# A graph network over 16 graphs: the nodes' transpose moved from TensorE to VectorE's 32x32 blocks

## The chip, the core and the metric

The kernel runs on one core of a Trainium2 chip. The metric is the device time of one execution in microseconds (us); lower is better. A core has five engines that run their own instruction queues in order: TensorE (PE, matrix products, with weight loads shown apart as PEld), VectorE (DVE), ScalarE (ACT), GpSimd (POOL) and SyncE (SP, which here only issues transfers). They wait for one another by semaphores.

## What is computed

For each of 16 graphs there are 1024 nodes with 256 features (x, fp32) and a symmetric adjacency matrix of 1024 x 1024 (int32, here 0 or 1, with ones on the diagonal). Layer 0 gates the sum over neighbours by a sigmoid of a weighted product of the nodes; layer 1 is graph attention with four heads. After each layer the input is added and the rows are normalised.

```python
h = hidden
e0 = leaky(einsum('bid,bjd->bij', h * a0[:, 0], h))      # e1, e2, e3 alike, for adj 2, 3, 4
alpha = sigmoid(where(adj == 1, e0, neg_inf))
x = layernorm(x + einsum('bij,bjd->bid', alpha, h) + bias)

Wh = (x @ W).reshape(B, N, H, F)                         # H = 4, F = 64
e = leaky_relu(e_src[:, :, None, :] + e_dst[:, None, :, :], 0.2)
alpha = softmax(where(mask, e, NEG_INF), axis=2)
x = layernorm(x + elu(einsum('bijh,bjhf->bihf', alpha, Wh)))
```

Since the adjacency is symmetric and holds only 0 and 1, the fast path uses e0 alone and computes only the upper half of the scores; a check at the end of the program falls back to a general path if the data don't allow this. The general path isn't taken with these inputs.

## The kernel before

Rows of 1024 nodes are held as 8 blocks of 128 partitions, features as two chunks of 128. The product of all nodes with all nodes needs x twice: with nodes on the partitions (tile xb, also the operand of the aggregation) and with features on the partitions (tile xT). The way from one to the other is what changes.

A graph is a set of stages, Python generators inside `stages` that issue one step at each `next`. In order of a graph's data:

- `xload` (L248) loads xb, `aload` (L258) the adjacency by blocks; `cast` (ScalarE) makes it bf16, `turn` (L281) transposes it (by transfer from SP, except in the first graph), `mask` (ScalarE) keeps it as bytes (mT).
- `xt` (L311) turns xb on TensorE: 16 transposes of 128x128 (L319) into four PSUM banks. `xtc` (L324) copies each bank to xT on ScalarE (L330). `xta` (L336) multiplies by a0 (ScalarE, L344).
- `score` (L352, products at L356), `leak` and `leaky` (slope 0.2, ScalarE L368 and VectorE L376), `sigmoid` (ScalarE L382), `below` and `lower` (L395, L401: mirror the upper half), `upper` (L412), `self_loop` (L419).
- `agg` (L423, products at L427), `residual` (L459), row statistics, `norm0` (ScalarE L489), `yt` (transposes L498), `ytc` (ScalarE L507), `project` (L513, L517), `wh` (ScalarE).
- `top_dve` and `top_pe` find a common maximum; the first step of top_dve (span, L560) reads all that wh has copied. `exps`, `product`, `high` and `low` make the factors (gm); `sload` (L644) brings the rows of sources (sbc).
- `pos` (L654, VectorE L658) makes a 0/1 matrix per head and block, 64 steps a graph; `acc` (products at L670) and `total` (L713) sum over it; `acc_low` (ScalarE L685) and `acc_sum` (VectorE L693) empty PSUM; then division, ELU (ScalarE L816), join, second normalisation and `leave` (store).

What sets the order on each engine is a table written out: TIMES gives each stage's steps a time in a graph's own count, FIRST and LAST do so for the first and last graph. `issue` (L1229) adds PERIOD (112.0) times the graph's number, sorts all steps, and issues them in that order. The units are a plan's, not measured microseconds; only the order counts, as every engine runs its queue in order. So three graphs are in flight at a time: scores of the next graph, attention of this one, the finish of the one before.

Buffers that matter: xb has two (pool f_io), xT one that it shares with yT (pool f_big), PSUM four banks for pt, e, agg, pw, pg, tot and the like (f_ps_t) and two double banks for acc, pos six.

```python
for b, stages in enumerate(graphs):
    table = FIRST if b == 0 else LAST if b == len(graphs) - 1 else TIMES
    for name, times in table.items():
        steps += [(b * PERIOD + at, stages[name]) for at in times]
for _, stage in sorted(steps, key=lambda step: step[0]):
    next(stage)
```

Of the kernel before, what the change touches and what calls it, by code (L numbers as in the profile page):

```python
# [27 lines left out]
P = 128  # L28
# [4 lines left out]
class Consts:  # L33
    pass

# [50 lines left out]
def transposed(nc, k, pl, src, name, copy, tag=None):  # L86

    dstT = pl.big.tile([P, k.DC, k.N], F32, tag=tag or name, name=name)
    for c in range(k.DC):
        for g in range(k.NH):  # L90
            pt = pl.ps_t.tile([P, 4, P], F32, tag="pt", name="pt")
            for q in range(4):
                nc.tensor.transpose(pt[:, q, :], src[:, 4 * g + q, c * P : (c + 1) * P], k.ident)
            copy(
                dstT[:, c, g * HALF : (g + 1) * HALF], pt.rearrange("p q n -> p (q n)")
            )
    return dstT
# [96 lines left out]
def stages(nc, k, pl, b, xg, adjg, outg, sums, span, zinv):  # L194
# [26 lines left out]
    def setup():  # L221
# [7 lines left out]
        nc.sync.dma_start(out=k.w_aug[:, :, 0:D], in_=w.rearrange("(c p) f -> p c f", p=P))  # L229
# [11 lines left out]
        for i in range(1, NK):  # L241
            nc.sync.dma_start(
                out=k.a_sb[:, :, i : i + 1], in_=a_list[i].rearrange("(c p) o -> p c o", p=P)
            )
# [3 lines left out]
    def xload():  # L248
# [7 lines left out]
        yield  # L256

# [53 lines left out]
    def xt():  # L311
        if first:

            t["acol"] = bank("acol")
            nc.tensor.transpose(t["acol"][:, 0:DC], k.a_row, k.ident[0:DC, 0:DC])
        for c, half in PARTS:
            pt = t["xt", c, half] = quads("pt")
            for q in range(NQ):
                nc.tensor.transpose(  # L319
                    pt[:, q, :], t["xb"][:, half * NQ + q, c * P : (c + 1) * P], k.ident  # L320
                )
            yield

    def xtc():  # L324
        t["xT"] = pl.big.tile([P, DC, N], F32, tag="xT", name="xT")
        if first:
            nc.vector.tensor_copy(k.a_sb[:, :, 0], t["acol"][:, 0:DC])
        for c, half in PARTS:
            copy = nc.vector.tensor_copy if first and c == 0 else nc.scalar.copy
# [163 lines left out]
    def yt():  # L493
        for half in range(NH):
            for c in range(DC):
                pt = t["yt", half, c] = quads("pt")
                for q in range(NQ):
                    nc.tensor.transpose(  # L498
                        pt[:, q, :], t["y", half][:, q, c * P : (c + 1) * P], k.ident
# [370 lines left out]
    def leave():  # L870
# [11 lines left out]
        setup=setup(), xload=xload(), aload=aload(), cast=cast(), turn=turn(), mask=mask(),  # L882
# [20 lines left out]
    "xload": [-190.36],  # L903
    "aload": [-141.21, -134.94, -129.14, -126.41, -107.72, -95.92, -52.91, -49.35],
    "cast": [-133.33, -126.54, -110.85, -106.42, -72.33, -55.28, -40.89, -29.41],
    "turn": [-133.00, -118.97, -108.09, -86.35, -62.89, -45.14, -38.49, -26.07],
    "mask": [-126.25, -118.09, -94.06, -70.56, -52.12, -40.03, -32.69, -25.15],
    "setup": [-54.43, -50.76, -47.38],
    "xt": [-69.63, -66.83, -65.59, -61.38],
    "xtc": [-65.35, -64.69, -63.96, -57.76],  # L910
    "xta": [-60.02, -56.47, -53.23, -47.62, -40.80, -39.84, -35.73, -22.45],
    "score": [
        -55.95, -54.26, -52.86, -52.85, -50.30, -47.61, -41.77, -41.05, -37.61, -36.60,
        -31.53, -19.69,
    ],
    "leak": [
        -54.25, -52.28, -52.05, -51.99, -45.24, -41.19, -38.48, -36.59, -34.23, -28.07,
        -26.47, -19.19,
    ],
    "leaky": [  # L920
        -53.92, -51.61, -45.43, -45.41, -41.52, -40.38, -37.19, -36.20, -32.91, -26.88,
        -25.80, -17.05,
    ],
    "sigmoid": [-50.37, -36.56, -28.45, -23.28, -23.17, -15.81, -5.09, 4.38],
    "below": [-43.48, -40.73, -36.17, -28.75, -25.55, -24.80, -21.22, -11.11, 7.22, 7.95],
    "lower": [-41.97, -37.35, -33.23, -27.18, -24.41, -23.38, -19.01, -9.26, 8.37, 17.62],
    "upper": [-24.74, -21.21, -20.88, -18.06, 1.37, 12.57, 17.16, 22.61],
    "self_loop": [-22.52, -20.95, -18.10, -17.88, 3.26, 14.07, 18.13, 24.49],
    "agg": [
        -18.25, -16.27, -15.06, -15.02, -4.11, -4.03, -2.54, 0.32, 5.09, 8.13, 15.85,  # L930
        17.47, 21.46, 23.59, 23.78, 24.56,
    ],
    "residual": [-8.35, -7.46, -1.27, 2.37, 22.46, 22.48, 26.43, 27.74],
    "moments0": [-5.49, -4.53, 5.61, 8.01, 23.75, 25.11, 27.16, 28.13],
    "gathered0": [4.13, 6.42, 7.91, 10.51, 26.40, 27.32, 28.51, 29.05],
    "spread0": [13.40, 31.26],
    "shift0": [17.29, 31.54],
    "norm0": [21.66, 21.89, 22.47, 23.38, 34.53, 34.91, 35.50, 35.54],
    "yt": [27.46, 27.57, 36.68, 36.99],
    "ytc": [29.00, 29.33, 39.29, 39.57],  # L940
    "project": [32.52, 32.60, 33.90, 39.19, 40.28, 40.33, 40.41, 40.81],
    "wh": [33.22, 36.59, 37.58, 40.10, 40.68, 42.17, 42.34, 43.12],
    "sources": [41.16, 45.78],
    "rows": [41.83, 54.07],
    "keep_rows": [44.82, 56.53],
    "top_dve": [43.38, 45.01, 45.39, 50.81, 51.81],
    "top_pe": [44.42, 46.92],
    "exps": [51.81],
    "product": [53.02, 53.37, 53.98, 54.66, 58.34, 66.43, 69.20, 72.08],
    "high": [53.76, 54.40, 58.33, 58.56, 61.32, 68.49, 71.81, 73.63],  # L950
    "low": [54.19, 57.97, 61.74, 62.89, 71.04, 72.63, 75.29, 76.96],
    "sload": [50.80, 79.07, 83.92, 88.62, 102.34, 116.17, 128.36, 142.07],
    "pos": [
        57.31, 58.08, 60.13, 63.67, 69.85, 70.05, 71.57, 77.68, 80.69, 81.39, 82.09,
        82.79, 83.51, 84.84, 85.08, 85.50, 94.75, 97.25, 97.29, 97.48, 99.31, 100.22,
        100.86, 101.86, 104.39, 105.08, 105.66, 107.42, 108.55, 108.94, 109.06, 109.44,
        111.06, 112.18, 112.18, 112.50, 114.43, 114.99, 117.57, 118.23, 118.61, 122.99,
        125.51, 126.22, 128.00, 128.98, 130.58, 132.32, 133.80, 134.68, 135.40, 135.59,
        136.35, 141.70, 144.45, 144.66, 145.90, 146.60, 148.13, 149.39, 151.16, 153.05,
        156.93, 159.83,  # L960
    ],
    "acc": [
        66.06, 67.27, 68.14, 69.24, 71.32, 72.44, 73.71, 78.80, 83.16, 83.97, 84.72,
        85.39, 85.74, 87.50, 88.94, 90.52, 99.28, 99.52, 100.60, 101.24, 101.47, 101.85,
        102.15, 102.38, 108.43, 108.66, 109.45, 109.46, 109.72, 110.12, 110.70, 110.77,
        114.66, 115.11, 115.34, 116.25, 116.73, 118.20, 118.35, 119.33, 130.24, 130.46,
        130.54, 131.53, 132.09, 132.57, 134.85, 134.91, 141.46, 142.49, 142.93, 144.35,
        145.14, 145.81, 145.91, 146.87, 153.97, 154.83, 159.23, 159.59, 164.73, 165.20,
        165.32, 166.33,
    ],  # L970
    "acc_low": [
        79.49, 79.83, 96.76, 97.23, 103.47, 104.76, 112.24, 112.31, 122.02, 122.21,
        134.93, 135.59, 149.34, 149.98, 169.77, 170.85,
    ],
    "acc_sum": [
        80.66, 80.96, 97.10, 98.04, 105.15, 105.96, 112.53, 112.54, 127.47, 127.48,
        136.59, 136.70, 149.39, 150.00, 171.97, 175.58,
    ],
    "all_edges": [
        24.35, 76.79, 79.33, 79.88, 81.06, 82.66, 85.63, 89.08, 96.83, 101.38, 102.99,  # L980
        108.02, 111.52, 113.15, 116.96, 118.15,
    ],
    "total": [
        77.14, 77.24, 78.75, 79.22, 79.40, 79.41, 79.97, 80.39, 84.60, 84.83, 85.08,
        85.73, 89.40, 89.80, 90.91, 93.34, 97.93, 100.95, 101.71, 106.58, 107.02, 107.21,
        109.68, 110.76, 112.06, 113.36, 114.66, 114.68, 117.04, 118.18, 118.28, 119.92,
    ],
    "total_kept": [80.79, 83.22, 90.91, 93.71],
    "total_less": [112.64, 113.12, 119.31, 124.40],
    "weigh": [119.49, 129.29, 190.71, 191.25, 196.08, 212.23],  # L990
    "divide": [
        125.16, 126.39, 127.60, 129.50, 130.49, 134.23, 134.70, 134.85, 200.68, 201.14,
        206.69, 213.74, 214.56, 214.57, 216.22, 218.60,
    ],
    "elu": [133.27, 142.72, 214.93, 220.17],
    "join": [136.57, 142.87, 142.93, 145.63, 220.24, 222.78, 225.82, 228.23],
    "moments1": [146.58, 148.42, 152.65, 153.15, 223.48, 227.82, 229.78, 230.58],
    "gathered1": [146.81, 150.62, 154.63, 154.74, 228.81, 229.65, 230.64, 230.81],
    "spread1": [164.98, 232.04],
    "shift1": [165.77, 237.22],  # L1000
    "norm1": [195.74, 197.90, 202.92, 203.03, 238.05, 240.07, 240.16, 240.29],
    "leave": [206.44, 240.93],
    "weigh_end": [222.86, 228.40],
    "divide_end": [222.94, 223.01, 223.09, 223.17, 228.57, 228.75, 228.92, 229.09],
    "elu_end": [223.25, 229.26],
    "join_end": [223.32, 223.40, 229.44, 229.61],
}
FIRST = {
    "aload": [-146.50, -146.40, -145.60, -145.40, -145.20, -144.50],
    "cast": [-146.00, -145.00, -144.10, -143.30, -142.40, -141.30, -140.80, -140.10],  # L1010
# [467 lines left out]
```

## Time and profile before

| what | value |
|---|---|
| median of 3 runs | 1741.87 us (1741.26 to 1742.15) |
| span of the profiled execution, first to last instruction | 1739.6 us |
| median of the runs less that span | 2.27 us |
| TensorE busy | 1692.1 us, 97% |
| VectorE busy | 1639.6 us, 94% |
| ScalarE busy | 1239.4 us, 71% |
| GpSimd busy | 106.8 us, 6% |
| mean granted TensorE clock | 0.990 |
| share of the 16 DMA engines' time, SP's queue | 36.1% |

The page gives no other time of the profiled execution than its span; what lies around the span is taken from the runs. Groups in the profile are lines of the kernel: engine, operation, output<-inputs, shapes, count, then busy time and mean duration of one instruction, then the idle time of the engine before them and who ended it. A wait line reads: engine, tile and line that waited, what it waited for, then the sum in us, how many times, and the longest. Busy time is the union of instructions that overlap, so a mean duration is longer than the pace at which the instructions follow each other. The ends of matrix products are modelled, so that a busy TensorE can also hide short waits; the chain of waits and the list of waits say more there.

### The profile page before, as it was taken

Reading aid. Unit: us, or ns where it says so; the run is one execution under the profiler, and the core shown is the slowest. Engines: PE = TensorE matmul, PEld = TensorE weight load, DVE = VectorE, ACT = ScalarE, POOL = GpSimd, SP = SyncE. Lnnn points to the kernel's source line nnn. Section 1 sums busy time; section 2 is a strip of 40 time slices with the busy share of each in tenths; the row PEclk is TensorE's granted clock in tenths of the full one; section 3 lists DMA queues with packets and bytes.
Section 4 is the critical chain, followed back from the end, with each engine's and each line's share of the span. In section 5 each row is a group of like instructions: output and inputs, shape, how many; then the busy total and the mean of one; then the engine's idle time right before and its main releaser. Section 6 shows DMA issues by size and latency. Waiting matters only on the chain.

```text
span 1739.6 us, 29647 instructions
## 1 busy us (share of the span) xinstructions
PE 1692.1 (97%) x10580; PEld 1492.5 (86%) x10580; DVE 1639.6 (94%) x3663; ACT 1239.4 (71%) x2766; POOL 106.8 (6%) x138
## 2 busy tenths in 40 slices
PE   8999999999999999999999999999999999999984
PEld 5789898998979889898998979889898898979883
DVE  5498999999999999999999999999999999999998
ACT  7674957759587685967759587685967859586784
POOL 0000000010000101000010000101000010000100
PEclk9999999999999999999999999999999999999987
DMA  5542333434334343333435334443343424422020
GB/s 190 129 116 67 98 98 92 110 92 131 88 89 101 105 125 92 94 101 92 109 92 129 91 86 102 105 128 91 89 107 92 110 67 117 105 71 55 26 68 26
DMA packets 249005, 168.59 MB, mean 97 GB/s; under 512 B 133010, under 2 KB 232468, under 8 KB 248852
## 3 DMA queue, kind: packets, MB, share of 16 engines
q1 hardware_dynamic: 248848, 166.63, 36.1%
q8 instruction: 86, 1.41, 0.3%
q14 instruction: 67, 0.55, 0.1%
q10 hardware_dynamic: 4, 0.00, 0.0%
HBM read 118.10 MB, written 17.04 MB: 78 GB/s over the span
## 4 chain that ended last, share of the span: by engine, by line
PE 91%; DVE 3%; ACT 2%; DMA 1%; issue 1%; POOL 0%; SPq 0%; ACTq 0%; DVEq 0%; POOLq 0%
PE acc L670 27%; PE agg L427 24%; PE tot L713 14%; PE e L356 13%; PE pw L517 7%; PE pg L395 3%; PE pt L498 2%; PE pt L319 1%; DVE pos L658 1%; DMA sbc<-sdram 1%; ACT prod L614 0%; DMA aT<-a 0%; PE pbc L591 0%; ACT gm L633 0%; ACT y L489 0%
## 5 line engine op out<-in xcount | busy, mean ns | idle before, releaser
L658 DVE SCALAR_TENSOR_TENSOR pos<-sbc,nd,mT 128x512 fp32r<-128x512 f32 x1024 | 737.4, 745 | 10.5 <-PE acc L670 5.0
L670 PE MATMUL acc<-gm,pos 128*128 128x260 f32 x4096 | 608.6, 292 | 8.9 <-DVE gm L640 5.0
L670 PEld LDWEIGHTS acc<-gm,pos 128*128 128x128 f32 x4096 | 536.8, 190 | 19.8 <-issue 5.7
L427 PE MATMUL agg<-xb,gate 128*128 128x256 f32 x2048 | 463.5, 379 | 0.2
L427 PEld LDWEIGHTS agg<-xb,gate 128*128 128x128 f32 x2048 | 379.9, 190 | 47.6 <-DVE gate L419 1.2
L713 PE MATMUL tot<-gm,allm 128*128 128x264 f32 x2048 | 328.8, 297 | 5.4 <-ACT gm L633 4.9
L713 PEld LDWEIGHTS tot<-gm,allm 128*128 128x128 f32 x2048 | 281.4, 189 | 9.7 <-ACT gm L633 5.1
L356 PE MATMUL e<-xT,xTa 128*128 128x512 f32 (+3 forms) x768 | 264.3, 489 | 2.2 <-ACT xTa L344 1.4
L356 PEld LDWEIGHTS e<-xT,xTa 128*128 128x128 f32 x768 | 135.1, 191 | 106.4 <-issue 55.3
L685 ACT COPY low<-acc 128x260 f32<-128x260 f32 x256 | 89.8, 377 | 187.5 <-PE acc L670 187.3
L705 ACT CAST allm<-mT 128x512 fp32r<-128x512 uint8 x256 | 157.4, 615 | 33.4 <-PE tot L713 31.7
L489 ACT ACTIVATE y<-y,shift,rstd 128x256 f32<-128x256 f32 x254 | 136.3, 592 | 48.6 <-DVE shift L477 48.6
L276 ACT ACTIVATE a<-a 128x1024 bf16<-128x1024 int32 x124 | 131.3, 1059 | 32.1 <-DMA aT<-a 23.0
L298 ACT ACTIVATE mT<-aT 128x1024 uint8<-128x1024 bf16 x120 | 127.1, 1059 | 7.6 <-DMA aT<-a 7.5
L468 POOL TENSOR_SCALAR std<-mv 128x4 f32<-128x4 f32 x64 | 27.7, 432 | 1618.7 <-DVE mv L450 1447.1
L517 PE MATMUL pw<-w_aug,yT 128*128 128x264 f32 x512 | 121.8, 387 | 0.5 <-ACT yT L507 0.5
L376 DVE TENSOR_TENSOR gate<-e,gate 128x512 f32<-128x512 f32 x192 | 105.5, 556 | 14.5 <-ACT gate L368 14.4
L693 DVE TENSOR_TENSOR u<-acc,low 128x260 f32<-128x260 f32 x256 | 103.1, 425 | 10.5 <-ACT low L685 10.3
L444 DVE BATCH_NORM_STATS2 st<-y 128x6 f32<-128x256 f32 x256 | 107.5, 421 | 1.2
L517 PEld LDWEIGHTS pw<-w_aug,yT 128*128 128x128 f32 x512 | 93.4, 190 | 15.4 <-ACT yT L507 1.9
L368 ACT ACTIVATE gate<-e 128x512 f32<-128x512 f32 x192 | 90.2, 486 | 13.7 <-PE e L356 13.3
L412 DVE TENSOR_TENSOR gate<-gate,mT 128x1024 f32<-128x1024 f32 (+7 forms) x128 | 96.6, 755 | 2.9 <-ACT mT L298 2.4
(111 smaller groups left out, 1788.8 us busy)
## 6 DMA issues: line engine op xcount, KB each, us to landing
a<-in_adj_dram SPq DMA_DIRECT2D x124, 512.0 KB, 4.6
sbc<-sdram SPq DMA_DIRECT2D x128, 256.0 KB, 4.6
out_dram<-y SPq DMA_DIRECT2D x31, 512.0 KB, 3.5
xb<-in_x_dram SPq DMA_DIRECT2D x15, 1024.0 KB, 5.4
a_us<-in_adj_dram SPq DMA_DIRECT2D x4, 512.0 KB, 8.9
aT<-a SPq DMA_TRANSPOSE x120, 3.1
xb<-in_x_dram SPq DMA_DIRECT2D x2, 512.0 KB, 4.7
sdram<-srow SPq DMA_DIRECT2D x32, 8.0 KB, 1.4
```

The lines of the kernel that those rows point to most:

```text
L276: nc.scalar.activation(t["a16", ib], t["a32", ib], AF.Copy, accum_out=sums[:, 0, at : at + 1])
L298: nc.scalar.activation(t["mT"][:, :, ib * P : (ib + 1) * P], t["aT", ib], AF.Square, accum_out=sums[:, 1, at : at + 1],)
L356: nc.tensor.matmul(e[:, 0:n], lhsT=t["xTa", jb][:, c, :], rhs=t["xT"][:, c, at : at + n], start=(c == 0), stop=(c == DC - 1),)
L376: nc.vector.tensor_tensor(ge, t["e", jb, at][:, 0:n], ge, ALU.max)
L427: nc.tensor.matmul(agg[:, 0:D], lhsT=t["gate"][:, jb, ib * P : (ib + 1) * P], rhs=t["xb"][:, jb, :], start=(jb == 0), stop=(jb == NB - 1),)
L444: nc.vector.bn_stats(st, t["y", half][:, q, :])
L489: nc.scalar.activation(y, y, AF.Identity, bias=shift, scale=rstd)
L517: nc.tensor.matmul(pw[:, 0:WD], lhsT=t["yT"][:, c, jb * P : (jb + 1) * P], rhs=k.w_aug[:, c, :], start=(c == 0), stop=(c == DC - 1),)
L658: nc.vector.scalar_tensor_tensor(p_, t["sbc", half, h], t["nd"][:, jb, h : h + 1], t["mT"][:, jb, half * HALF : (half + 1) * HALF], ALU.is ...
L670: nc.tensor.matmul(t["acc", half, h, q // 2][:, q % 2, 0 : 2 * E], lhsT=t["pos", half, h, jb][:, q * P : (q + 1) * P], rhs=pl.gm[:, h, jb] ...
L705: nc.scalar.copy(m_, t["mT"][:, j0 : j0 + 4, ib * P : (ib + 1) * P])
L713: nc.tensor.matmul(tot[:, 0 : H * F1], lhsT=t["allm", ib, jb // 4 * 4][:, jb % 4, :], rhs=pl.gm[:, :, jb, l, F:E], start=(jb == 0 and l == 0),
```

## The change

The first graph keeps its way. For graphs 2 to 16 `xt` is no longer issued at all. A new stage `x2load` loads x a second time, into a tile x2 that shares xb's two buffers: four transfers, one for each 32 partitions (QB = 32), each with 32 x 32 runs of 64 features. Partition 32 b + q of x2 holds, for each group a of 32 nodes, 64 neighbouring features of node 32 a + q. `xtc` then has two steps instead of four, both on VectorE: one transpose instruction in blocks of 32x32 over 128 partitions and 1024 elements, which takes every second feature (c = 0 or 1) and writes chunk c of xT.

With that, chunk c holds the features 2 p + c on partition p instead of 128 c + p. So that all operands agree, the loads of W and of a1 to a3, the row a0 and every TensorE transpose of features (`chunk`) take every second column too. `xload` moves to a later place, as xb now only serves the aggregation. All three tables are new; of these, the lines of TIMES that the text speaks of are shown.

```diff
--- before.py
+++ after.py
@@ -32,6 +32,14 @@
 
 class Consts:
     pass
+
+
+QB = 32
+
+
+def chunk(row, c, parts):
+
+    return row.rearrange("p (n c) -> p c n", c=parts)[:, c]
 
 
 def shapes(x, a_src):
@@ -90,7 +98,7 @@
         for g in range(k.NH):
             pt = pl.ps_t.tile([P, 4, P], F32, tag="pt", name="pt")
             for q in range(4):
-                nc.tensor.transpose(pt[:, q, :], src[:, 4 * g + q, c * P : (c + 1) * P], k.ident)
+                nc.tensor.transpose(pt[:, q, :], chunk(src[:, 4 * g + q, :], c, k.DC), k.ident)
             copy(
                 dstT[:, c, g * HALF : (g + 1) * HALF], pt.rearrange("p q n -> p (q n)")
             )
@@ -226,7 +234,7 @@
         rows = two("vecs")
         for row, a in zip(rows, (a_src, a_dst)):
             nc.sync.dma_start(out=row, in_=a.rearrange("h f -> (h f)").partition_broadcast(P))
-        nc.sync.dma_start(out=k.w_aug[:, :, 0:D], in_=w.rearrange("(c p) f -> p c f", p=P))
+        nc.sync.dma_start(out=k.w_aug[:, :, 0:D], in_=w.rearrange("(p c) f -> p c f", p=P))
         yield
 
         for which in range(2):
@@ -240,7 +248,7 @@
         nc.sync.dma_start(out=k.bias_bc, in_=bias.partition_broadcast(P))
         for i in range(1, NK):
             nc.sync.dma_start(
-                out=k.a_sb[:, :, i : i + 1], in_=a_list[i].rearrange("(c p) o -> p c o", p=P)
+                out=k.a_sb[:, :, i : i + 1], in_=a_list[i].rearrange("(p c) o -> p c o", p=P)
             )
         yield
 
@@ -254,6 +262,18 @@
                 out=t["xb"][:, c, :], in_=xg.rearrange("(c p) d -> p c d", p=P)[:, c, :]
             )
         yield
+
+    def x2load():
+        if first:
+            yield from (None for _ in range(P // QB))
+            return
+        t["x2"] = pl.io.tile([P, N // QB, QB * DC], F32, tag="xb", name="x2")
+        for i in range(P // QB):
+            nc.sync.dma_start(
+                out=t["x2"][i * QB : (i + 1) * QB],
+                in_=xg.rearrange("(a q) (b e) -> b q a e", q=QB, e=QB * DC)[i],
+            )
+            yield
 
     def aload():
         for ib in range(NB):
@@ -312,12 +332,15 @@
         if first:
 
             t["acol"] = bank("acol")
-            nc.tensor.transpose(t["acol"][:, 0:DC], k.a_row, k.ident[0:DC, 0:DC])
+            for c in range(DC):
+                nc.tensor.transpose(
+                    t["acol"][:, c : c + 1], chunk(k.a_row, c, DC), k.ident[0:1, 0:1]
+                )
         for c, half in PARTS:
             pt = t["xt", c, half] = quads("pt")
             for q in range(NQ):
                 nc.tensor.transpose(
-                    pt[:, q, :], t["xb"][:, half * NQ + q, c * P : (c + 1) * P], k.ident
+                    pt[:, q, :], chunk(t["xb"][:, half * NQ + q, :], c, DC), k.ident
                 )
             yield
 
@@ -325,8 +348,16 @@
         t["xT"] = pl.big.tile([P, DC, N], F32, tag="xT", name="xT")
         if first:
             nc.vector.tensor_copy(k.a_sb[:, :, 0], t["acol"][:, 0:DC])
+        if not first:
+            for c in range(DC):
+                nc.vector.transpose(
+                    t["xT"][:, c, :].rearrange("p (a q) -> p a q", q=QB),
+                    t["x2"].rearrange("p a (r c) -> p c a r", c=DC)[:, c],
+                )
+                yield
+            return
         for c, half in PARTS:
-            copy = nc.vector.tensor_copy if first and c == 0 else nc.scalar.copy
+            copy = nc.vector.tensor_copy if c == 0 else nc.scalar.copy
             copy(
                 t["xT"][:, c, half * HALF : (half + 1) * HALF],
                 t["xt", c, half].rearrange("p q n -> p (q n)"),
@@ -496,7 +527,7 @@
                 pt = t["yt", half, c] = quads("pt")
                 for q in range(NQ):
                     nc.tensor.transpose(
-                        pt[:, q, :], t["y", half][:, q, c * P : (c + 1) * P], k.ident
+                        pt[:, q, :], chunk(t["y", half][:, q, :], c, DC), k.ident
                     )
                 yield
 
@@ -879,7 +910,7 @@
             yield
 
     return dict(
-        setup=setup(), xload=xload(), aload=aload(), cast=cast(), turn=turn(), mask=mask(),
+        setup=setup(), xload=xload(), x2load=x2load(), aload=aload(), cast=cast(), turn=turn(), mask=mask(),
         xt=xt(), xtc=xtc(), xta=xta(), score=score(), leak=leak(), leaky=leaky(),
         sigmoid=sigmoid(), below=below(), lower=lower(), upper=upper(), self_loop=self_loop(), agg=agg(),
         residual=residual(), moments0=moments("0"), gathered0=gathered("0"),
@@ -900,329 +931,328 @@
 
 PERIOD = 112.0
 TIMES = {
...
-    "xload": [-190.36],
-    "aload": [-141.21, -134.94, -129.14, -126.41, -107.72, -95.92, -52.91, -49.35],
-    "turn": [-133.00, -118.97, -108.09, -86.35, -62.89, -45.14, -38.49, -26.07],
-    "setup": [-54.43, -50.76, -47.38],
-    "xt": [-69.63, -66.83, -65.59, -61.38],
-    "xtc": [-65.35, -64.69, -63.96, -57.76],
-    "xta": [-60.02, -56.47, -53.23, -47.62, -40.80, -39.84, -35.73, -22.45],
+    "xload": [-22.60],
+    "x2load": [-139.53, -99.31, -94.40, -66.12],
+    "aload": [-172.98, -115.62, -105.65, -96.09, -75.97, -62.00, -46.47, -34.23],
+    "turn": [-111.58, -103.55, -89.47, -63.86, -56.74, -45.75, -33.02, -20.52],
+    "setup": [-36.81, -26.35, -26.35],
+    "xtc": [-48.18, -47.57],
+    "xta": [-47.10, -45.77, -41.30, -36.41, -33.58, -29.82, -28.10, -5.07],
...
-    "sigmoid": [-50.37, -36.56, -28.45, -23.28, -23.17, -15.81, -5.09, 4.38],
+    "sigmoid": [-25.70, -23.08, -16.04, -14.06, -3.81, 18.73, 25.12, 27.58],
...
-    "residual": [-8.35, -7.46, -1.27, 2.37, 22.46, 22.48, 26.43, 27.74],
...
-    "yt": [27.46, 27.57, 36.68, 36.99],
-    "project": [32.52, 32.60, 33.90, 39.19, 40.28, 40.33, 40.41, 40.81],
...
-    "top_dve": [43.38, 45.01, 45.39, 50.81, 51.81],
-    "top_pe": [44.42, 46.92],
-    "exps": [51.81],
...
+    "residual": [5.36, 12.19, 13.66, 19.97, 44.19, 46.64, 49.04, 51.61],
...
+    "yt": [44.87, 48.32, 55.77, 55.77],
+    "project": [52.88, 54.38, 54.38, 57.42, 60.46, 62.17, 62.17, 62.17],
...
+    "top_dve": [63.86, 64.59, 64.59, 66.30, 66.30],
+    "top_pe": [64.30, 65.45],
+    "exps": [67.72],
...
-    "elu": [133.27, 142.72, 214.93, 220.17],
+    "elu": [154.66, 162.65, 231.56, 240.45],
...
@@ -1393,8 +1423,8 @@
             stages(nc, k, pl, b, x[b], adj[b], out[b], sums, span, zinv) for b in range(B)
         ]
         k.a_sb = const.tile([P, k.DC, NK], F32, name="a_sb")
-        k.a_row = const.tile([k.DC, P], F32, name="a_row")
-        nc.scalar.dma_start(out=k.a_row, in_=a0.rearrange("(c p) o -> c (p o)", p=P))
+        k.a_row = const.tile([1, D], F32, name="a_row")
+        nc.scalar.dma_start(out=k.a_row, in_=a0.rearrange("d o -> o d"))
         for name in ("xload", "aload", "aload"):
             next(graphs[0][name])
         with tc.tile_pool(name="first", bufs=1) as first:
```

## The prediction, made blind

> **What bounds the kernel now.** I read the windows first, because a mean over the whole span mixes the fill, fourteen like periods and the drain. In the chain of waits, agg blocks of 32 instructions start at 743.44, 847.88 and 952.32: 104.44 us a graph. The windows, at round borders and then cut at this period:
>
> ```profile
> core 0: us, PE busy (x) PEld busy (x) DVE busy (x) ACT busy (x) POOL busy (x), PEclk, DMA share, GB/s
> 0.00:112.00 112.00, 100.83 (x523) 75.29 (x524) 66.06 (x159) 83.67 (x177) 3.80 (x14) 1.00 0.51 145
> 112.00:217.00 105.00, 105.00 (x663) 93.21 (x662) 94.94 (x202) 66.47 (x152) 5.43 (x6) 1.00 0.35 94
> ...
> 1575.00:1740.00 165.00, 128.93 (x869) 121.46 (x867) 151.40 (x369) 103.50 (x299) 10.80 (x14) 0.89 0.14 41
> ```
> ```profile
> 739.40:843.90 104.50, 104.50 (x660) 92.70 (x659) 102.29 (x227) 76.05 (x167) 6.60 (x8) 1.00 0.37 99
> 843.90:948.30 104.40, 104.40 (x659) 92.60 (x658) 102.24 (x227) 75.95 (x167) 6.60 (x8) 1.00 0.39 100
> ...
> sum 417.80, PE 417.77 PEld 370.33 DVE 408.48 ACT 303.83 POOL 26.39; mean PE 104.44 PEld 92.58 DVE 102.12 ACT 75.96 POOL 6.60
> ```
>
> In the steady periods TensorE is busy all of 104.44 us at the full granted clock (1.00). VectorE is busy 102.12, so only 2.3 us a graph stand between it and the bound. ScalarE has 28 us spare. Only the first two windows show a VectorE with real idle time (46 and 10 us); the drain (1575 on) is VectorE's, 151.4 of 165.
>
> A busy TensorE could still be one that waits, so next the chain of waits over four steady periods, and the waits there:
>
> ```profile
> by line: PE acc L670 29.5%; PE agg L427 26.5%; PE tot L713 15.4%; PE e L356 14.8%; PE pw L517 6.8%; PE pg L395 3.0%; PE pt L498 1.7%; PE pt L319 1.7%; PE pbc L591 0.3%; PE ps L541 0.2%; PE ptop L588 0.1%; issue 0.0%
> ```
> ```profile
> ACT xT L330 <- PE pt L319: 3.3, 8, 0.4
> DVE u L693 <- ACT low L685: 3.0, 4, 0.7
> ...
> DVE gate L376 <- ACT gate L368: 1.5, 3, 0.5
> DVE shift L477 <- POOL rstd L469: 1.3, 4, 0.3
> DVE pos L658 <- DMA sbc<-sdram: 1.1, 1, 1.1
> ```
>
> The steady chain is TensorE from end to end. VectorE's named waits are small and belong to ScalarE, GpSimd and a load.
>
> **What is removed.** Sixteen transposes a graph (L319) for graphs 2 to 16, and ScalarE's four copies out of PSUM (L330):
>
> ```profile
> L319 PE MATMUL pt<-ident,xb 128*128 128x128 f32 x256 | 37.5, 282 | 2.4 <-DMA xb<-in_x_dram 2.4
> L330 ACT COPY xT<-pt 128x512 f32<-128x512 f32 x62 | 34.6, 585 | 16.8 <-PE pt L319 16.8
> ```
>
> The 282 ns of one transpose overlap with the next. The price on TensorE is the start-to-start pace: in the steady period 739 to 844, L319's 16 instructions hold 1.69 us (106 ns each), and the chain gives them 1.7%, 1.77 us. I take 1.69: TensorE would need 102.75 us a graph. ScalarE sheds 4 x 0.585 = 2.34 us; it isn't on the path.
>
> **What is added to VectorE.** Two 32x32-block transposes a graph, each 1024 elements in every partition, fp32, read with every second element. No row shows a VectorE transpose. Nearest are the 1024-element instruction and the one single-source copy:
>
> ```profile
> L412 DVE TENSOR_TENSOR gate<-gate,mT 128x1024 f32<-128x1024 f32 x16 | 19.6, 1225 | 2.5 <-ACT mT L298 2.4
> L330 DVE COPY xT<-pt 128x512 f32<-128x512 f32 x2 | 1.4, 691 | 3.5 <-PE pt L319 3.4
> ```
>
> [...] From above: half the rate, the 1225 ns plus another 1.07 (the rows of 1024 and 512 elements differ by 1225 - 683 = 542 ns for 512), 2.3 us. [...] Consecutive instructions overlap. In the four steady periods VectorE's 226 instructions a graph sum to 120.5 us but fill 102.1, 0.081 us less each; the timeline starts the next one 1.13 us after a 1.23 us L412. So the two cost 2 x 1.14 = 2.28 us a graph (1.2 to 4.4).
>
> [...]
>
> **The new balance.** VectorE's floor before is 120.5 - 226 x 0.085 = 101.3 us, if every instruction overlaps as those in unbroken runs do. After: 101.3 + 2.28 = 103.6. TensorE: 102.75. VectorE becomes the bound, and the floor is only 0.84 us under today's period. What decides is how much idle time a bound VectorE keeps. Before, it had 104.44 - 101.3 = 3.1 us above its floor, part of it mere slack behind TensorE. Its named waits in the steady window are 3.0 + 1.5 + 1.3 + 1.1 = 6.9 us in four graphs, 1.7 each. ScalarE gets lighter: the copies above, and table loads. The sigmoid (L382) and exponential (L816, L598) calls stand in the old table so that their kinds change six times a period, in the new one four times; 43 and 42 loads of 1283 ns in the page agree with about six. That is 2 x 1.28 = 2.6 us, so 4.9 us in all off ScalarE. That should shorten waits for ScalarE but not those for GpSimd, loads or TensorE. I take 1.5 us of idle: a period of 105.1, 0.66 above 104.44.
>
> **Other edits.** The x2 loads: four DMAs a graph, 256 KB each in runs of 256 bytes, 4096 packets on some 15,500 a graph (248,848 / 16). By the mean packet time the DMA share goes from 36% to about 46%; by bytes (1 MB on 10.4) to 40%. [...] SP pays 4 x 0.37 = 1.5 us of issue (xb's row has 372 ns) and passes them in line with the adjacency loads, turns, sload and leave. The last x2 load stands at -66.1 in the table, its transpose at -48.2: 18 table units, about 17 us, against a landing of 5.4. If late, VectorE's whole queue stands behind it (top_dve, product, low, pos) and TensorE's scores with it. The xT buffer (one, shared with yT) makes the first VectorE transpose wait for TensorE's last project (62.2 in its own graph's time, the transpose 63.8). But the same place of VectorE's queue waits anyway for ScalarE's copies of that projection (span L560, which follow project), so I cost it at nothing; without that cover it is one project call, 4 x 0.21 = 0.8 us. The xb load moves from -190 to -22.6, 19 units ahead of its first use in agg: covered. It shares its two buffers with x2; each one's predecessor is finished over 20 units earlier.
> Chunks of every second column: 16 weight loads a graph for yt (L498) now read at a stride of 8 bytes. No row shows a strided load of weights; from nothing to a doubled pace (+1.7 us), I take nothing, as a bound VectorE leaves TensorE 2.3 us (105.1 - 102.75). Setup loads and the first graph's one more tiny transpose: under a microsecond once, within the fill's uncertainty.
> The tables: between the last project and the first acc, TensorE has 8 acc calls and 8 score calls in the new order against 8 acc, 4 xt and 6 score before, 14.5 against 14 us by the same paces. The pipeline's depth is alike. I see no hole in the order, but a whole-looking order can lose or win in fill and drain; I allow 6 us either way, a tenth of VectorE's 56 us of idle time in the fill.
>
> **Sum.** The two early periods, where TensorE is the bound and VectorE has idle time: 2 x -1.69 = -3.4. Thirteen periods at +0.66: +8.6. Net +5.2: the profiled execution's span of 1739.6 becomes 1744.8. The runs' median, 1741.87, lies 2.27 above that span (start and end that the span leaves out), so I forecast 1747, +0.3%. Differences within 0.2% (3.5 us) can't be told from no change by measurement.
>
> **Rivals.**
> *VectorE packs tightly.* The idle time before was slack behind TensorE; with 4.9 us less on ScalarE, VectorE keeps 0.3 us. Period 103.9: 13 x -0.54 - 3.4 = -10.4, so 1731. It decides at an idle of 0.84 + 3.4/13 = 1.1 us: below that the change gains. For it: named waits half ScalarE's; the planner filled TensorE to 100.0%. Against: a second engine, TensorE, would be within 1% of full too, and each waits for the other through six pos and four PSUM buffers.
> *The transpose is slow.* Half rate, or the stride costs it: +2.1 us a graph more, period 107.2, 13 x 2.8 - 3.4 = +33: 1775. For it: no row with a strided fp32 read of this length. [...]
> *VectorE keeps its 3.1 us, or a transpose stalls for project or x2.* Period 106.7: +26, so 1768.
> *The change doesn't relieve TensorE* (strided weight loads give 1.7 back): TensorE 104.4, VectorE 103.6 + 1.5, both full; 0.5 to 1 us more a period and no early gain, 1757 to 1763.
>
> **Chances.** Forecast 1747 (own range 1738 to 1757) 0.40; tight packing 0.25; kept idle or stall 0.17; strided weights 0.08; slow transpose 0.10. Of tight packing four fifths are faster by over 0.2%, the rest within; of the forecast's own spread a third lies within 0.2%, and nearly all else above: faster 0.22, same 0.18, slower 0.60. The range runs from tight packing (1731, less a little fill) to the slow transpose (1775) with a share of the fill: 1729 to 1780.
>
> **What would show it.** VectorE busy 103.5 us or more of the steady period and TensorE no longer filling it, with TensorE waiting for pos, gate or u; the transposes at about 1.23 us, L319's count down to 16; six table switches down to four. I am wrong if TensorE's busy time still equals the period, if the transposes take 0.7 or 2.3 us, if VectorE's idle time is under 1.1 us a graph, or if fill and drain move by over 6 us.

## The result, and the profile after

The changed kernel takes 1773.45 us (median of 4 runs, 1771.32 to 1774.51) against 1741.93 before: a ratio of 1.0183, 95% interval 1.0168 to 1.0197. It is slower, inside the forecast's range but 26 us above the forecast itself of 1747. Its profiled span is 1769.5 us, 29.9 more than before.

The windows of the changed kernel, cut at its period, answer to those cut at 104.44 us. The columns are as before; the period is 106.48 us now.

```profile
683.19:789.66 106.47, 104.86 (x643) 91.52 (x642) 103.90 (x229) 72.36 (x160) 5.69 (x8) 1.00 0.46 109
789.66:896.14 106.48, 104.90 (x643) 91.53 (x642) 103.93 (x229) 72.39 (x160) 5.69 (x8) 1.00 0.46 110
...
sum 638.87, PE 629.22 PEld 548.97 DVE 623.49 ACT 434.31 POOL 34.15; mean PE 104.87 PEld 91.49 DVE 103.91 ACT 72.38 POOL 5.69
```

TensorE no longer fills its period (104.87 of 106.48), and VectorE doesn't either (103.91): neither is busy throughout. And TensorE's busy time in a period has not fallen with its 16 transposes but risen from 104.44; the forecast had 102.75. The 2.04 us that a period grew, times fifteen, is 30.6 us, so the whole loss is in the steady periods; fill and drain together changed by less than a microsecond (1739.6 - 15 x 104.44 = 173.0 before, 1769.5 - 15 x 106.48 = 172.3 after).

The groups of the changed kernel that answer to the lines shown before:

```profile
L353 DVE STREAM_TRANSPOSE xT<-x 128x1024 f32<-128x1024 f32 x30 | 36.6, 1223 | 0.0
L529 PEld LDWEIGHTS pt<-ident,y 128*128 128x128 f32 x256 | 35.7, 205 | 0.9
L413 ACT ACT_TABLE_LOAD x31 | 39.8, 1283 | 0.6
```

A transpose takes 1223 ns (1225 forecast). The table loads at L413 fell from 43 to 31. The weight loads of yt, which now read every second column, take 205 ns; before it was 141.

The acc products of both kernels, before and after, over the whole span:

```profile
L670 PE MATMUL acc<-gm,pos 128*128 128x260 f32 x4096 | 608.6, 292 | 8.9 <-DVE gm L640 5.0
L701 PE MATMUL acc<-gm,pos 128*128 128x260 f32 x4096 | 633.8, 299 | 26.2 <-DVE pos L689 14.9
```

The same products hold TensorE 25 us longer, and it waits 17 us more ahead of them, most of it for VectorE's pos. In four steady periods they go from 152.1 us and no idle time ahead of them to 158.3 us and 4.6 us: 2.7 us a graph, more than the 1.69 that the transposes gave.

The waits over four steady periods of the changed kernel (the line of the waiter, what it waited for, sum, times, longest):

```profile
...
PEld acc L701 <- DVE pos L689: 4.9, 9, 1.0
DVE shift L508 <- POOL rstd L500: 4.6, 4, 1.2
...
DVE u L786 <- PE tot L744: 4.0, 4, 1.0
...
PE acc L701 <- DVE pos L689: 3.0, 4, 0.8
...
PE pbc L622 <- DVE dtop L600: 1.6, 4, 0.4
```

Before, no wait of a matrix product showed in the steady window. Now the products wait for pos (acc) and for dtop (pbc), while VectorE waits 1.15 us a graph for rstd and 1.0 for tot. That both wait suggests that the bound changes hands within each period. The chain of waits through one period of the changed kernel (start, length, what) shows where, with most pieces left out:

```profile
789.66 3.45 PE agg L458 x16
...
810.43 2.40 PE acc L701 x20
812.83 0.14 PE pt L529
812.97 0.05 issue
813.02 0.80 DVE pos L689 x2
...
819.61 1.13 DVE xT L353
820.74 0.11 DVE span L591
...
821.10 1.15 DVE xT L353
822.26 0.17 DVE topT L597
...
894.67 0.67 DVE pos L689
895.35 0.04 issue
895.39 0.76 PE acc L701 x4
```

For 23 us, from 789.7 to 813.0, TensorE is the last in everything: agg, acc, total, yt and projection. From there to 895.4 it is VectorE, and then TensorE takes over as one pos arrives. Both of VectorE's long waits (at 799.8 for tot and 810.2 for rstd) lie in TensorE's stretch. Both transposes stand soon after the hand-over, around the search for the common maximum: the steps span to top need the last copies of the projection, topT needs TensorE's ptop.

By this chain alone, the theory would be the forecast's: VectorE has 2.28 us more to do, keeps its idle time, and the period grows. A rival is that the new order costs, another that the strided weight loads do. The runs decide between them.

### The profile page after: what moved, and what is told of

Same layout as the page of the kernel before. It is cut to its first block, busy times and chain, and to the rows that moved or that the text cites. A ratio compares the mean times of both kernels' runs of the same rounds, so it can differ in the third digit from the quotient of the medians.

```text
span 1769.5 us, 29077 instructions
## 1 busy us (share of the span) xinstructions
PE 1699.4 (96%) x10341; PEld 1479.8 (84%) x10341; DVE 1667.8 (94%) x3693; ACT 1190.0 (67%) x2682; POOL 93.3 (5%) x138
## 4 chain that ended last, share of the span: by engine, by line
DVE 60%; PE 25%; issue 12%; ACT 1%; POOL 1%; DMA 1%; DVEq 0%; SPq 0%; POOLq 0%; ACTq 0%
DVE pos L689 23%; PE agg L458 11%; PE acc L701 7%; DVE gate L407 4%; DVE gm L671 4%; DVE gate L443 4%; DVE prod L650 4%; DVE gate L432 3%; DVE u L724 3%; DVE st L475 3%; PE pw L548 2%; DVE u L803 2%; PE tot L744 2%; DVE xT L353 2%; DVE u L821 1%
## 5 line engine op out<-in xcount | busy, mean ns | idle before, releaser
L689 DVE SCALAR_TENSOR_TENSOR pos<-sbc,nd,mT 128x512 fp32r<-128x512 f32 x1024 | 719.7, 740 | 1.7 <-PE acc L701 1.5
L701 PE MATMUL acc<-gm,pos 128*128 128x260 f32 x4096 | 633.8, 299 | 26.2 <-DVE pos L689 14.9
L701 PEld LDWEIGHTS acc<-gm,pos 128*128 128x128 f32 x4096 | 544.4, 191 | 71.0 <-DVE pos L689 17.8
L458 PE MATMUL agg<-xb,gate 128*128 128x256 f32 x2048 | 470.0, 379 | 0.1
L744 PE MATMUL tot<-gm,allm 128*128 128x264 f32 x2048 | 315.1, 296 | 3.5 <-ACT gm L664 2.4
L387 PE MATMUL e<-xT,xTa 128*128 128x512 f32 (+3 forms) x768 | 269.2, 492 | 3.8 <-ACT xTa L375 3.0
L520 ACT ACTIVATE y<-y,shift,rstd 128x256 f32<-128x256 f32 x254 | 134.1, 591 | 108.3 <-DVE shift L508 108.2
L499 POOL TENSOR_SCALAR std<-mv 128x4 f32<-128x4 f32 x64 | 17.3, 270 | 1662.2 <-DVE mv L481 1459.6
L475 DVE BATCH_NORM_STATS2 st<-y 128x6 f32<-128x256 f32 x256 | 99.8, 410 | 1.2
L399 ACT ACTIVATE gate<-e 128x512 f32<-128x512 f32 x192 | 85.5, 476 | 15.9 <-PE e L387 15.9
L375 ACT ACTIVATE xTa<-xT,a_sb 128x128 f32<-128x128 f32 x240 | 82.4, 391 | 20.0 <-DVE xT L353 20.0
```

Of the source, the lines that this page charges most:

```text
L387: nc.tensor.matmul(e[:, 0:n], lhsT=t["xTa", jb][:, c, :], rhs=t["xT"][:, c, at : at + n], start=(c == 0), stop=(c == DC - 1),)
L458: nc.tensor.matmul(agg[:, 0:D], lhsT=t["gate"][:, jb, ib * P : (ib + 1) * P], rhs=t["xb"][:, jb, :], start=(jb == 0), stop=(jb == NB - 1),)
L475: nc.vector.bn_stats(st, t["y", half][:, q, :])
L520: nc.scalar.activation(y, y, AF.Identity, bias=shift, scale=rstd)
L689: nc.vector.scalar_tensor_tensor(p_, t["sbc", half, h], t["nd"][:, jb, h : h + 1], t["mT"][:, jb, half * HALF : (half + 1) * HALF], ALU.is ...
L701: nc.tensor.matmul(t["acc", half, h, q // 2][:, q % 2, 0 : 2 * E], lhsT=t["pos", half, h, jb][:, q * P : (q + 1) * P], rhs=pl.gm[:, h, jb] ...
```

## The experiments

Each ratio is to the kernel before, run on the same chip (its medians 1741.8 to 1742.7). Periods are between the same instructions of steady graphs in each trace.

**One part at a time: the stride, the move, the order.**

The first run takes the tables and the turn of before, and only lets chunks take every second column, for all 32 feature transposes a graph:

```diff
-    pt[:, q, :], t["xb"][:, half * NQ + q, c * P : (c + 1) * P], k.ident
+    pt[:, q, :], chunk(t["xb"][:, half * NQ + q, :], c, DC), k.ident
```

> Only the chunks take every second column (weights, a, and all of TensorE's feature transposes, 32 a graph, read at a stride of 8 bytes); the turn stays on TensorE, the order is that of before. Theory (VectorE's queue is what costs): nothing but the slower weight loads seen in the changed kernel's yt (205 against 141 ns, mostly hidden), 1742 to 1750. Rival (strided weight loads take the gain back): 1.7 us for 16 transposes and twice that for 32, so 1765 or more.

Measured: 1748.12 us, ratio 1.0032 (1.0020 to 1.0043), period 104.81. Loads go from 141 to 206 ns, but 32 of them cost only 0.37 us a period. The rival falls as the main cost: 5.4 us, where it expected 1765 us or more. The changed kernel has 16 such loads a graph, and there TensorE isn't the bound throughout.

The second run makes the move in the old tables. The new loads and the two transposes are put in by hand:

```diff
-    "xload": [-190.36],
+    "xload": [-40.00],
+    "x2load": [-110.00, -100.00, -90.00, -84.00],
-    "xt": [-69.63, -66.83, -65.59, -61.38],
-    "xtc": [-65.35, -64.69, -63.96, -57.76],
+    "xtc": [-65.35, -64.69],
```

> The turn on VectorE with its loads, in the tables of before (x2 loads and the xb load put in by hand, the two transposes at the old places of the first two copies). Theory: VectorE gets 2.28 us more a period and is bound, period 106 to 107, 1763 to 1778, as in the changed kernel. Rival (the new order is what costs): near the forecast for a well-packed order, 1740 to 1750.

Measured: 1767.07 us, ratio 1.0144 (1.0127 to 1.0161), period 106.0. It came out as the theory expected, and in its chain both transposes stand in full, between the last projection and the next scores:

```profile
822.36 2.35 DVE xT L353 x2
```

The third run takes the new tables with the turn left on TensorE; the four steps of xt and of xtc go to where VectorE's transposes stood, no x2 is loaded, and the load of xb goes to -75:

```diff
-    "xtc": [-48.18, -47.57],
+    "xt": [-48.188, -48.187, -48.182, -48.181],
+    "xtc": [-48.184, -48.183, -48.178, -48.177],
```

> The new tables with the turn still on TensorE (its 16 transposes and ScalarE's four copies issued where VectorE's two transposes stand, between the last projection and the next scores), no x2 loads. Theory: VectorE is as light as before, so TensorE is the bound again, 104.5 to 105.5 a period, 1742 to 1757. Rival (the new order is what costs): period stays near 106.5, 1765 or more.

Measured: 1800.16 us, ratio 1.0334 (1.0317 to 1.0351), period 108.2. That is far outside what the theory expected: with less work on VectorE than the changed kernel, the new order is 27 us slower than it. In the old order the move loses 19 us (1748 to 1767), in the new one it wins 27 (1800 to 1773), and with TensorE's turn the new order alone loses 52. Both mixed kernels have steps placed by hand, so these are no clean prices of an order; but they rule out that the move costs the same wherever it stands. In the third run the place itself costs much: the 16 transposes stand just ahead of ptop in TensorE's queue, and VectorE's topT waits for ptop (sum over four periods, times, longest):

```profile
DVE topT L589 <- PE ptop L611: 15.3, 4, 3.8
```

That is 3.8 us a graph. What it would be without the transposes there, the next run shows.

**VectorE's transposes taken away.** ScalarE makes a plain copy of x2 in their place (the turning itself is left out):

```diff
-                nc.vector.transpose(
+                nc.scalar.copy(
                     t["xT"][:, c, :].rearrange("p (a q) -> p a q", q=QB),
```

> The changed kernel, but xT of graphs 2 to 16 is a plain copy of x2 by ScalarE in the place of VectorE's transposes: the turning itself is left out, everything else, loads included, stays. Theory: VectorE sheds 2.28 us a period, of which the period gives back 1.5 to 2.3 until TensorE's 102.8 to 104.9 stops it: 1739 to 1751. Rivals (the order, or the x2 loads, cost): within 6 us of the changed kernel's 1773.

Measured: 1771.85 us, ratio 1.0169 (1.0152 to 1.0186), period 106.25. Here the theory falls: VectorE shed two instructions of 1.22 us a graph and the kernel gained 1.6 us of 1773, 0.23 us in a steady period. In this run's waits over four periods a line appears that the changed kernel doesn't have:

```profile
DVE topT L597 <- PE ptop L619: 7.6, 4, 1.9
```

And its chain at the hand-over runs through TensorE to the ptop transpose:

```profile
821.72 0.82 PE acc L701 x4
822.55 0.11 PE ps L572
822.66 1.44 PE acc L701 x12
824.10 0.11 PE ps L572
824.21 0.12 PE ptop L619
824.33 0.02 issue
824.35 0.29 DVE topT L597
```

Without transposes VectorE stands at topT for 1.9 us a graph, since ptop is queued on TensorE behind 16 acc products. In the changed kernel's order the transposes fill just this gap. So their 2.28 us are nearly free there, and something else makes the period 106.3. ScalarE's copies aren't in the way: TensorE waits for its xTa 1.0 us in four periods here, 1.7 in the changed kernel.

Against the third run, VectorE's wait at topT halves, by 1.9 us a graph, and the period is 1.9 us shorter. So 28 of the 52 us above go with TensorE's transposes ahead of ptop; the other 24 remain with neither engine turning anything. They go with the order: the acc products take 630 to 635 us in all nine kernels with the new tables, also in this one (631.1) and in the third run without x2's loads (632.5), and 605 to 610 in all five with the old ones, also with VectorE's transposes and x2's loads (605.1).

**Twice the transposes,** each issued two times, to see what the gap leaves:

```diff
+                for _ in range(2):
                     nc.vector.transpose(
```

> The changed kernel with each of VectorE's two transposes issued twice (same output). New theory after the ScalarE copies gave nothing: the first pair lies in a gap in which VectorE would wait 1.9 us a graph for TensorE's ptop, so it is nearly free; a second pair finds no gap and costs its full 2.28 us a graph, 15 graphs, +34: 1800 to 1810. Rival (VectorE's work doesn't set the period at all): 1773 to 1780.

Measured: 1832.98 us, ratio 1.0523 (1.0506 to 1.0541). The second pair costs 59.5 us, 4.0 a graph, where the first cost 0.2 at most and 34 us had been expected. Work in front of topT was free here up to the gap of 1.9 us and then dearer than its own time of 2.28. The run's waits over four periods show where:

```profile
PE pbc L623 <- DVE dtop L601: 8.4, 4, 2.1
DVE gate L408 <- ACT gate L400: 6.1, 10, 0.8
PE ptop L620 <- DVE top L595: 2.8, 4, 0.7
```

TensorE, whose queue is in order, stops at ptop and pbc (2.8 us a graph) with its scores behind them, and VectorE then waits for the late scores' leak (1.5 us a graph). The granted TensorE clock was 0.98 in this run's steady windows, against 1.00 in the changed kernel's; how much of the 4.0 us that makes isn't shown.

**Work and waits elsewhere on VectorE.** First, shift is made by GpSimd behind its rstd, so that VectorE doesn't wait there:

```diff
-            nc.vector.scalar_tensor_tensor(shift, mvh[:, :, 0], -1.0, rstd, ALU.mult, ALU.mult)
+            nc.gpsimd.tensor_tensor(shift, mvh[:, :, 0], rstd, ALU.mult)
+            nc.gpsimd.tensor_scalar(shift, shift, -1.0, None, ALU.mult)
```

> The changed kernel with shift (L508, four small instructions a graph) made by GpSimd behind its rstd instead of by VectorE, so VectorE no longer waits 1.16 us a graph for rstd. Theory: that wait lies in the stretch in which TensorE is the bound, so VectorE only arrives earlier at its next wait; at most the gap's last 0.4 us and three tiny instructions come back: 1762 to 1776. Rival (the forecast's logic: any idle time of VectorE costs): 1.5 us a graph, 1751 or less.

Measured: 1775.19 us, ratio 1.0189 (1.0172 to 1.0206): nothing came back. It fits the theory of two stretches, but isn't clean: the normalisation waits longer behind GpSimd's two more instructions (35.2 us in four periods against 28.0). Next, the eight additions of the identity go to GpSimd:

```diff
-            nc.vector.tensor_tensor(own, own, k.ident, ALU.add)
+            nc.gpsimd.tensor_tensor(own, own, k.ident, ALU.add)
```

> The changed kernel with the eight additions of the identity (L450) on GpSimd instead of VectorE. They stand in the stretch in which VectorE is the bound. Theory: the period loses most of their 8 x 0.2 us until TensorE's own 104.9 stops it: 1747 to 1760. Rival (VectorE's work doesn't set the period): 1770 or more; GpSimd's own slowness could spoil it either way.

Measured: 1761.92 us, ratio 1.0112 (1.0095 to 1.0129): 11.5 us back, 0.8 a graph of the 1.6 or more taken off, just short of what was expected. VectorE's pos took 753 ns on average in four steady graphs, against 740 in the changed kernel: 64 x 0.013 = 0.8 us a graph, which would be the rest. That this is GpSimd's doing isn't shown, as pos took 750 ns with ScalarE's copies too. Third, four steps of TIMES are moved, to fill the two waits and bring two pos steps ahead of topT:

```diff
-    "shift0": [39.36, 53.98],
+    "shift0": [39.36, 54.77],
-    "norm0": [40.90, 40.90, 40.90, 40.90, 54.44, 54.44, 54.44, 54.67],
+    "norm0": [40.90, 40.90, 40.90, 40.90, 54.78, 54.78, 54.78, 54.785],
-    "total_less": [140.07, 142.92, 150.16, 157.06],
+    "total_less": [140.07, 142.92, 150.16, 158.61],
-        170.86, 177.74, 178.36,
+        170.86, 175.20, 176.00,
```

> The changed kernel with four steps of its TIMES table moved and nothing else: shift0's second and total_less's last step stand one or two pos steps later (VectorE's two waits of 1.16 and 0.98 us in TensorE's stretch are filled), and the last two pos steps of the graph before stand ahead of the topT step instead of behind it. Theory: 1.3 us of VectorE's work leaves the stretch in which it is the bound, into time in which it waited; period about 105, 1750 to 1760. Rival (some other chain sets the period): 1768 or more.

Measured: 1800.71 us, ratio 1.0340 (1.0323 to 1.0357), a clear miss. The last run repeats it without the last of these edits, the two pos steps:

> The changed kernel with only the two moves that fill VectorE's waits for rstd and tot (later places for one shift step and one total_less step), without the two pos steps ahead of topT that the earlier combined run also had (1801). Theory: the filled waits lie in TensorE's stretch and are worth no more than VectorE's 0.4 us lateness at topT: 1765 to 1776; so it was the two pos steps, which delay top and topT for which TensorE's queue waits, that cost the combined run 27 us. Rival (the later shift delays the normalisation, yt and the projection): 1785 or more.

Measured: 1762.89 us, ratio 1.0120 (1.0103 to 1.0136), period 105.8. Its waits show none for rstd and 0.3 us a graph for tot, so 1.8 us are filled. They give 10.6 us back, 0.7 a graph, more than expected, and the two pos steps in front of topT (1.3 us of work) lose 37.8, 2.5 a graph: again about twice their time (in the run that had them the granted clock was 0.98 to 0.99 in the steady windows, in this one 1.00). The waits of the run that had them, over four periods:

```profile
PE pbc L622 <- DVE dtop L600: 5.9, 4, 1.5
PEld ptop L619 <- DVE top L594: 4.5, 4, 1.1
DVE pos L689 <- PE acc L701: 3.6, 4, 0.9
PE ptop L619 <- DVE top L594: 3.3, 4, 0.8
```

The waits of ptop for top and of pos for acc don't show among those of the changed kernel, and pbc waited 0.4 us a graph there, not 1.5. The price of VectorE's time thus depends on the place: next to nothing in the gap, 0.7 of the 1.8 us of waits filled in TensorE's stretch, about half of what the identity's additions took, and about double in front of top and topT once the gap is full.

**Three of eight products on GpSimd,** in three kernels:

```diff
+                engine = nc.gpsimd if s and h else nc.vector
-                nc.vector.tensor_tensor(
+                engine.tensor_tensor(
                     prod, t["wh"]
```

The move in the old order:

> The turn on VectorE in the tables of before (as in the run with the move only, 1767), and three of the eight products a graph (L650, s = 1 of heads 1 to 3) on GpSimd instead of VectorE. In that run's chain each period has one stretch of 21 us in which VectorE is the bound, from the end of the projection to the next scores, and both transposes (2.35 us) and all products lie in it. Theory: taking 3 x 0.6 us out of this stretch gives most of it back, 14 periods: 1740 to 1750. Rival (VectorE's work in the stretch doesn't matter, or GpSimd's products come too late): 1764 or more.

Measured: 1766.02 us, ratio 1.0136 (1.0119 to 1.0153). The kernel before:

> The kernel before with the same three products on GpSimd, as a control. Theory: VectorE isn't the bound there, TensorE is: 1736 to 1746. Rival (any VectorE work taken off helps): 1725 or less.

Measured: 1742.02 us, ratio 0.9998 (0.9989 to 1.0006). The changed kernel:

> The changed kernel with the same three products on GpSimd. They stand in the 83 us stretch in which VectorE is the bound. Theory: 3 x 0.6 us a graph comes back until TensorE's 104.9 stops it, as with the additions of the identity (1762): 1747 to 1762. Rival (it was GpSimd's or the additions' place that mattered): 1768 or more.

Measured: 1773.46 us, ratio 1.0177 (1.0160 to 1.0194). Only the control came out as expected. The other two don't refute the stretches, since little work left VectorE: in the changed kernel with GpSimd's products, its remaining products went from 684 ns to

```profile
L651 DVE TENSOR_TENSOR prod<-wh,es 128x512 f32<-128x512 f32 x20 | 18.2, 946 | 0.0
```

which is 5 x 0.262 = 1.3 us a graph of the 1.8 that the three products had taken; VectorE's busy time in a period fell only from 103.9 to 103.5 us. Its pos went from 740 to 749 ns, but that needn't be GpSimd's doing, as they take 750 in the run with ScalarE's copies, where GpSimd has no new work. In the old order with the move, the gm instructions (L671) went from 691 to 747 ns and pos from 746 to 763, 8 x 0.056 + 64 x 0.017 = 1.5 us. Whether VectorE's work in the stretch behind topT has its full price there thus stays open; the additions of the identity, whose removal left it the clearest net relief, suggest that it has.

## Why the prediction was right, and which steps failed

The sign and the range held, the forecast of 1747 and the way to it did not. The range reached to 1780 for a slow transpose and for idle time kept, and the transpose wasn't slow; that 1773 lies inside is in part luck.

*TensorE's relief.* The 16 transposes are gone, but "TensorE: 102.75" failed: it is busy 104.87 us a period. In the new order the acc products take back 2.7 us a graph in busy time and waits, more than the 1.69 removed. The price of the transposes on TensorE isn't their pace of 106 ns alone either: the run with the turn on TensorE and the one with ScalarE's copies differ by 1.9 us a period (108.18 - 106.25), which is by how much ptop came later. (They differ in x2's loads and in the number of ScalarE's copies too.)

*The price of a transpose.* Right: 1223 ns for 1225. No run of before shows that term for a transpose, nor the low end of 0.7 us; 1225 ns, on which the 2.28 us rest, is the row of the plain 1024-element instruction (L412). The changed kernel's 30 transposes, fp32 and read at a stride of 8 bytes, took no longer than that.

*"The two cost 2.28 us a graph."* This step failed for the new order. There they stand in a gap of 1.9 us at topT, and taking them away gave 0.2 us a period. The forecast saw that VectorE's queue waits at this place for the copies of the projection, and used this only to cost the xT buffer's wait at nothing; the transposes themselves lie in the same cover. In the old order they stood on the chain in full.

*"I take 1.5 us of idle."* This is the mis-sized term. VectorE's busy time is 103.91, near the forecast's 103.6, but its idle time in the period is 2.57, against 2.3 before; over the floor of 103.6 the period has 2.9. The rival "keeps its 3.1 us" gave 106.7 a period, nearest to the measured 106.48, and 1768 us. The slow transpose, at 1775, is nearer in time, but its cause is refuted by the 1223 ns. The reason of the first wasn't quite the real one either: by the chain, TensorE is the bound in 23 us of each period, with both of VectorE's waits inside, and VectorE in the rest. A floor for one engine, worked out over the whole period, doesn't see this. Filling the two waits by order alone brought 10.6 of the 31.5 us back.

*"I see no hole in the order."* Failed as well, and most of the loss goes with it. The comparison of acc and score calls between projection and first acc gave 14.5 and 14 us, true but blind to what stands between: ptop and pbc, where the two queues meet in order. It also says nothing on how long acc waits for pos. The order was allowed 6 us either way; the kernel in which neither engine turns anything is still 24 us slower than the old order with strided loads and TensorE's turn.

*Fill and drain,* forecast at -3.4 from the early periods, gave -0.7. *The loads:* DMA share 0.46 in the steady window as forecast, landing of x2 5.3 us; nobody waits for them. *Strided weight loads:* taken at nothing; with 32 a graph and TensorE as bound they cost 5.4 us. *Table loads:* 61 now against 85, four a period as read from the tables.

What stays open is which steps of the new order make acc slower and later, and whether an order exists that uses the relief: none of the twelve kernels beats the one before, the nearest with VectorE's turn being 1762.

## What to carry to other kernels

Here two engines were each over 97% busy (104.87 and 103.91 of 106.48 us), and the period had no single bound: find in the chain where it changes hands, and price an instruction by the stretch and the queue position it gets, not by the engine's total. In a gap that a wait leaves, work was nearly free here until the gap was full (0.2 us a period for 2.28); past that it cost about double (4.0 for 2.28, 2.5 for 1.3), with the other engine's in-order queue stopped too. Moving work between such engines is only as good as the order that is made for it, so try the order with the old work and the work with the old order before crediting either, and look where the steps that you move by hand come to stand.

## What the runs showed of the hardware

A GpSimd product with two SBUF inputs went with a longer VectorE product beside it. The timeline of the changed kernel with three products on GpSimd:

```profile
838.16 1.07 POOL L651 TENSOR_TENSOR prod<-wh,es 128x512 f32<-128x512 f32 x1 [4.80 <-DVE gm L672]
838.33 1.44 DVE L651 TENSOR_TENSOR prod<-wh,es 128x512 f32<-128x512 f32 x1
```

VectorE's product takes 1.44 us there and 0.68 on average in the changed kernel, where no product is on GpSimd. The excess of 0.76 us is a little under the rest of GpSimd's instruction (838.16 + 1.07 - 838.33 = 0.90). Moving three products to an idle GpSimd thus gave VectorE little here: 1.8 us of products moved, 0.4 us less busy time.

A weight load of 128 x 128 fp32 that reads every second column took 206 ns instead of 141 in the run with the stride only, and cost 12 ns in pace there (0.37 us a period for 32).
